# A four-layer graph network in fp32: one pool of 40 places for seven kinds of 4-KB buffers, row sums into a junk tile, and a plan taken strictly by a new table of due times

## The chip, the cores and the metric

The kernel runs on one core of a Trainium2 chip. Its engines are TensorE (PE, with its weight loads listed apart as PEld), VectorE (DVE), ScalarE (ACT), GpSimd (POOL) and SyncE (SP), which here only issues DMAs. The metric is the device time of one execution in microseconds (us). Before the change it was 2382.04, 2384.33 and 2385.14 us in three runs, with the median at 2384.33.

## The reference

There are 16 graphs of N = 1024 nodes with D = 128 features in fp32. `adj` is a weighted 1024 x 1024 adjacency matrix per graph. Four layers follow one another, each of them a layernorm with relu, a graph operation and a residual:

```python
# layer 0, three times (b is 0): cosine-weighted adjacency
h = h @ W + b
nh = h / jnp.maximum(jnp.linalg.norm(h, axis=-1, keepdims=True), EPS)
ew = adj * jnp.einsum('bij,bkj->bik', nh, nh)
h = jnp.einsum('bpq,bqc->bpc', ew, h)            # relu but for the last
# layer 1
h = (1.0 + eps) * x + jnp.einsum('bnf,bnm->bmf', x, adj)
y = jnp.maximum(h @ W1 + b1, 0.0) @ W2 + b2
# layer 2: attention with tanh scores
alpha = jnp.tanh(s1[:, :, None] + s2[:, None, :])
attn = jax.nn.softmax(jnp.where(adj > 0, alpha, NEG_INF), axis=-1)
last_h = jnp.einsum('bij,bjf->bif', attn, h)     # node itself where the row sum of adj is 0
# layer 3: gated attention
e = jnp.einsum('bil,bkl->bik', h @ A, h); e = e + jnp.swapaxes(e, 1, 2)
att = jax.nn.softmax(jnp.where(adj > 0, e, 0), axis=1) * adj
h_prime = jax.nn.relu(jnp.einsum('bij,bjk->bik', att, h))
out = o_c * jnp.tanh(jax.nn.sigmoid(i_c * h_prime + f_c * x))   # i_c, f_c, o_c: gates of [x, h_prime]
```

## The kernel before, in words

**Tiling.** The nodes lie in NB = 8 blocks of 128. A full feature tile is 128 partitions x 1024 elements: node blocks side by side, or, transposed, features on the partitions. Each graph keeps its adjacency transposed as eight tiles `adjT` of 128 x 1024, and reads it once more untransposed as tiles `adjL` for layer 1. A 512-element half of a row is the unit of the large products.

**A square.** Layers 0 and 3 need a symmetric 1024 x 1024 product of features (`sq`, class `Square`, L1335 to L1425). `row` (L1363) multiplies only from the diagonal block on; the blocks below are mirrored by transposes (`sq<-ident,above`, L1373) out of blocks kept in SBUF. `keep` stores them: ScalarE copies (L1398), or VectorE transposes (L1385) for a far quarter. Where a square is "by DMA", `send` writes a far quarter to DRAM (`by_hbm`, L1412) and fetches it turned (`got`, L1422). The kept blocks of one square are a tile `above` of 22 blocks (11 KB per partition).

**The stages of one graph.** Loads: `x` (L1459), for graph 0 untransposed chunks `raw` (L1494) that TensorE transposes (L1172), for the other graphs four DMAs per tile that fill `adjT` in 32 x 32 squares (L1518), VectorE's transpose of them (L1526) and ScalarE's row sum (L1529, eight tiles a graph for 15 graphs: 120). Layer 0, sublayers 00, 01, 02: projection `psP` (L1203), norms (square on ACT L1575, sum on DVE L1581, power -0.5 on POOL L1165, called `rn`), features transposed (`ps_hTn` L1172, evicted to `hTn` by L1225), square, `ew = sq*rn*adjT` on VectorE (L1598), product `acc0` (L1431), evicted by ScalarE to `hT` of the next sublayer (L1225). Layer 1: `adjL` plus the scaled identity (L1643), product with `hn`, two dense products. Layer 2: scores on ScalarE (L1764 and L1768), times adjT on VectorE (L1772, `e2`), product by nodes (L1442, `acc2`), and `hrow`, `pf` (L1706, L1713) for nodes alone. Layer 3: mask (L1842), masked scores with the maximum (L1863, `e3`), exp (L1895), times adjT on VectorE (L1904) or, in the last two graphs, in part on POOL (L1900), values `hs` scaled by the sums (L1909, L1913), product, `hpT` and `psN`, the gates (to L2008) and the output (L2015).

**The order.** Nothing is issued as it is written down. Each `pe`, `act`, `dve`, `pool_op` or `op("DMA", ...)` records an `Op` with an estimated duration in a `Plan` (from L57 on), with what it reads and writes. `Plan.order()` (L138 to about L220) then lists all of them, and they are emitted in that list's order under a manual schedule, so each engine's queue is the part of the list that is its own. SP has one queue for nearly all DMAs. Each operation has a due time, `batch * PERIOD + TIMES[key][nth]`, from a long table by stage, engine and tile, with entries of its own for the first two graphs and the last two. PERIOD is 145.06. `order()` steps through simulated time: of the operations that are ready it finds the earliest start, takes the engine of that start, and on this engine the one with the smallest due time within WINDOW = 0.05 us. While a VectorE operation with two SBUF inputs is planned, POOL operations are held off, and the other way round (`port`).

**Places.** A `Buf` takes a place in a pool when its first writer is listed; the place is free when its last user is. POOLS gives the places: adjT 16, adjL 5 (raw too), x 3, big 13 (`w4` work tiles and `chunk`s), above 2, and smaller ones. KINDS gives each kind its pool, the most places it may hold at once and the most that graphs later than the oldest unfinished one may hold. A reused place makes the new writer wait for the old users on the chip.

Of the kernel before, what the change touches and what calls it, by code (L numbers as in the profile page):

```python
# [10 lines left out]
I8 = mybir.dt.int8  # L11
AF = mybir.ActivationFunctionType
ALU = mybir.AluOpType
AX = mybir.AxisListType
# [20 lines left out]
class Buf:  # L35


    def __init__(self, kind, shape, name):
        self.kind, self.shape, self.name = kind, shape, name
        self.slot = self.t = None  # L40
        self.uses = 0
        self.seen, self.users = [], []
        self.end = 0.0
# [12 lines left out]
class Plan:  # L56
# [78 lines left out]
    def order(self):  # L135
# [12 lines left out]
        rows = {e: i for i, e in enumerate(self.LATENCY)}  # L148
        while ready:
# [4 lines left out]
            found = []  # L154
            for o in ready:
                if o.batch > oldest + self.ahead and o.engine != "DMA":
                    continue
                at = max(free[o.engine], o.from_)
                if o.port and port > at:
                    at = port  # L160
                if o.new:
                    need, room = {}, {}
                    for b in o.new:
                        need[b.kind] = need.get(b.kind, 0) + 1
                    for k, n in need.items():
                        pool, most, share = self.kinds[k]
                        if total[k] + n > most or (o.batch > oldest and young[k] + n > share):
                            at = None
                            break
                        room[pool] = room.get(pool, 0) + n  # L170
                    if at is not None:
                        for pool, n in room.items():
                            if len(state[pool]) < n:
                                at = None
                                break
                            at = max(at, state[pool][n - 1][0])
                    if at is None:
                        continue
                found.append((at, o))
            if not found:  # L180
                stuck = [b.name for o in ready if o.batch == oldest for b in o.new]
                raise RuntimeError(f"no slot for any of {stuck}")
            first = min(found, key=lambda f: (f[0], rows[f[1].engine]))
            at, o = min(
                (f for f in found if f[1].engine == first[1].engine and f[0] <= first[0] + self.window),
                key=lambda f: f[1].rank,
            )
# [34 lines left out]
def tile_adj_preln(  # L222
# [45 lines left out]
    nc.vector.memset(half, 0.5)  # L268
    mhalf = const.tile([P, NB], F32, name="mhalf")
# [55 lines left out]
    for load_it in first:  # L325
# [11 lines left out]
    POOLS = {"adjT": 16, "adjL": 5, "x": 3, "big": 13, "above": 2, "got": 1, "bank": 8, "small": 29, "row": 6, "hbm": 3, "hrow": 2, "mask": 5, "dot": 12}  # L337
    KINDS = {
        "adjT": ("adjT", 16, 16), "adjL": ("adjL", 5, 5), "x": ("x", 3, 3), "w4": ("big", 9, 5),
        "chunk": ("big", 10, 12), "above": ("above", 2, 1), "got": ("got", 1, 1), "ps": ("bank", 7, 8),  # L340
        "acc": ("bank", 7, 8), "small": ("small", 7, 16), "row": ("row", 3, 3), "hbm": ("hbm", 3, 3),
        "hrow": ("hrow", 1, 1), "mask": ("mask", 5, 5), "dot": ("dot", 6, 11),
    }
    PERIOD, AHEAD, WINDOW = 145.06, 2, 0.05

    TIMES = {
        "T DMA raw <0": [51.6, -92.65, -42.9, 3.5, 39.85, 7.55, 4, 14.6],
        "T PE raw <0": [8.95, 14, 0.9, 0.1, 1.8, 11.5, 24.3, 8.7, 10.25, 24.85, 23.15, 30.8, 27.8, 31.75,
            37.1, 39.05],
        "T ACT adjT <0": [10.4, 39.05, 8.5, 13.4, 18.8, 14.95, 18.55, 20.55, 23.6, 34, 35.15, 28.45, 39.25,  # L350
            43.8, 44.95, 62.3],
        "T DVE su <0": [53.8],
        "x DMA x <0": [51.55, -93.7],
        "0 DVE st <0": [3.5, 4.1],
        "0 DVE mv <0": [9.55],
        "0 POOL rstd <0": [4.05],
        "0 DVE nb <0": [8],
        "0 DVE hn <0": [9],
        "0 ACT hn <0": [38.8],
        "0 PE ps <0": [0.3, 12.55],  # L360
        "0 ACT hT <0": [-29.95, 13.25],
        "00 PE psP <0": [-4, -11.9],
        "00 DVE h <0": [12.3, 13.05],
        "00 PE ps <0": [23.7, 4.25],
        "00 ACT hTn <0": [15.5, 15.95],
        "00 ACT sq <0": [9.5, 16.45],
        "00 DVE ss <0": [-0.4, 17.4, 18.1],
        "00 POOL rn <0": [31.75],
        "00 PE sq <0": [5.9, 23.6, 7.2, 24.25, 13.15, 8.2, 10.5, -25.2, 6.35, 35.5, 21.75, 22.95, 30.8,
            27.05, 27.75, 40.9, 34.6, 52.3, 47.45, 25.15, 52.8, 47.65],  # L370
        "00 ACT above <0": [16.8, 25.9, 20.15, 21.45, 21.05, 27.1, 27, 35.15, 44.25, 39.55],
        "00 DVE ew <0": [20.55, 22.4, 22.5, 36.85, 24.55, 30.55, 38.4, 34.95, 29.5, 42.65, 33.2, 41.35, 48.7,
            51.6, 44.75, 54.3],
        "00 PE acc0 <0": [1.15, 16.5, 13, 10.35, 16.8, 17.8, 23.5, 23.4, 29.8, 44.65, 39.75, 41, 36.25,
            62.05, 45.45, 57.85],
        "00 POOL params <0": [36.5, 32.1, 45.3, 53, 56.95, 59.45, 57.95],
        "00 DMA params <0": [51.15],
        "00 DVE params <0": [65.55, 68.05, 68.05, 72.5, 77.85],
        "00 PE params <0": [46.25, 59.4, 67.2],
        "00 ACT hT <0": [71.35, 58.35],  # L380
        "01 PE psP <0": [48.7, 58.7],
        "01 DVE h <0": [69.85, 69.8],
        "01 PE ps <0": [62.15, 55.8],
        "01 ACT hTn <0": [74.6, 77.8],
        "01 ACT sq <0": [88.4, 75.85],
        "01 DVE ss <0": [76.35, 76, 75.35],
        "01 POOL rn <0": [85.7],
        "01 PE sq <0": [69.35, 77.1, 67.35, 71.05, 69.5, 61.9, 71.9, 72.55, 83.05, 79.35, 79.85, 82.25,
            81.65, 86.95, 89.5, 88.15, 86.6, 87.9, 88.85, 85.6, 88.85, 80.2],
        "01 ACT above <0": [84.55, 78.6, 81.55, 80.85, 88.55, 86.7, 99.05, 90.1, 98.25, 100.1],  # L390
        "01 DVE ew <0": [78.05, 92.3, 81.45, 86.7, 87.75, 96.2, 92.9, 91.6, 93.85, 100.95, 89.4, 98.6, 96.4,
            111.05, 92.4, 91.6],
        "01 PE acc0 <0": [73.8, 85.1, 79.95, 79.7, 80.75, 79.35, 85.55, 82.95, 86.65, 87, 85.75, 88.7, 88.55,
            92.6, 90.25, 95.7],
        "01 ACT hT <0": [102.35, 105.3],
        "02 PE psP <0": [93.5, 94.1],
        "02 DVE h <0": [111.55, 105.55],
        "02 PE ps <0": [95.75, 93.15],
        "02 ACT hTn <0": [114.45, 109.95],
        "02 ACT sq <0": [139.5, 103.55],  # L400
        "02 DVE ss <0": [110.85, 118.05, 110.75],
        "02 POOL rn <0": [132.95],
        "02 PE sq <0": [104.2, 101.25, 108.75, 111.1, 102.75, 106.15, 102.05, 93, 108.8, 109.9, 109.8, 115.1,
            115.55, 112.1, 119.5, 119.95, 122.9, 111.5, 118.6, 122.3, 121.85, 129.35],
        "02 ACT above <0": [114.75, 122.65, 108.55, 121.65, 119, 120.9, 125.85, 129.8, 136.8, 145.15],
        "02 DVE ew <0": [113.15, 105.5, 117.9, 112.35, 125.6, 119.95, 118.75, 124.8, 129.8, 126.4, 126.55,
            132.7, 131.6, 126.8, 122.9, 141.5],
        "02 PE acc0 <0": [115.6, 116.45, 107.95, 105, 109.15, 114.05, 117.4, 112.55, 132.75, 118.2, 123.05,
            131.2, 113.55, 121.5, 124.25, 117],
        "02 DVE x <0": [137.5, 138.95],  # L410
        "T DMA adjT <1": [-127.65, -137.2, -158.65, -112.3, -198.45, -149.5, -107.65, -98.7],
        "T DVE adjT <1": [-118.5, -112.1, -110.7, -105.6, -102, -90.25, -86.2, -85.25],
        "T ACT adjT <1": [-112.4, -112.9, -110.15, -106.5, -87.15, -73.4, -90.65, -89.55],
        "1 DVE st <0": [135.85, 142.2],
        "1 DVE mv <0": [141.85],
        "1 POOL rstd <0": [135.1],
        "1 DVE nb <0": [144.4],
        "1 DVE hn <0": [140.7],
        "1 ACT hn <0": [139.15, 139.6],
        "1 DVE x <0": [143.2, 166.35, 170],  # L420
        "1 DMA adjL <0": [51.6, 65.9, 63.85, 62.15, 49.9, 160.9, 153.9, 153.25],
        "1 DVE adjL <0": [80.75, 72.65, 82.35, 76.45, 78.15, 151.65, 156.4, 161.25],
        "1 PE acc1 <0": [135.6, 136.4, 137.3, 138.1, 140.45, 138.5, 143.45, 140.85, 143.9, 142.2, 148.6,
            147.5, 149.25, 146.5, 153.05, 144.3],
# [1712 lines left out]
```

## Time and profile before

| what | value |
|---|---|
| profiled execution | 2384.38 us |
| its span, first to last instruction | 2382.6 us |
| mean granted TensorE clock | 0.996 |
| median of three runs | 2384.33 us |
| DMA moved | 314.31 MB, mean 132 GB/s |
| largest group, DVE L1598 `ew<-sq,rn,adjT`, 612 x 739 ns | 439.2 us |
| row sums, ACT L1529, 120 x 1055 ns | 126.5 us |
| POOL power L1165 `rstd`, 64 x 1660 ns | 106.2 us |

The span is 1.8 us shorter than the execution's own time. A group's line of the profile has the source line, the engine, the operation and the tiles, the number of instructions, their busy time and mean, and then the engine's idle time just before them with what ended most of it. The slices of the span by tenths show the same level through the run except at its ends:

```profile
PE   8999999999999999999999999999999999999997
...
DVE  6658798998988989899898989989899898887676
ACT  7325765756566565765756567465765756655375
```

Each digit is one fortieth of the span (59.6 us).

### The profile page before, as it was taken

To read this page: it belongs to the slowest core of one execution; us is meant where nothing else is said; L and a number is where in the kernel's file an instruction comes from. 1 tells how busy PE (TensorE), PEld (TensorE's weight loads), DVE (VectorE), ACT (ScalarE), POOL (GpSimd) and SP (SyncE) were. 2 spreads that over 40 slices of the span, in tenths; PEclk is the share of its full clock that TensorE was granted. 3 is DMA by queue.
4 is the path that set the end of the run, shared out by engine and by line. 5 is a ranking of instruction groups with operands and counts; after the bars stand their busy time and mean duration, and the time that the engine had idled before them with its cause. 6 is when DMAs were issued, how large, how long until landed. Compare 5 with 4: busy or idle time off the path is not lost.

```text
span 2382.6 us, 35138 instructions
## 1 busy us (share of the span) xinstructions
PE 2346.0 (98%) x11577; PEld 1552.4 (65%) x11577; DVE 2038.7 (86%) x5570; ACT 1435.5 (60%) x2561; POOL 247.7 (10%) x168
## 2 busy tenths in 40 slices
PE   8999999999999999999999999999999999999997
PEld 5568566675757657566675766757576575765764
DVE  6658798998988989899898989989899898887676
ACT  7325765756566565765756567465765756655375
POOL 3001010100101101010100101001011100100012
PEclk9999999999999999999999999999999999999999
DMA  9332938668585875949769496775948768165000
GB/s 195 88 107 63 177 92 185 149 135 167 123 177 138 148 168 130 178 109 183 156 125 183 108 181 142 146 168 132 164 129 164 160 128 158 49 112 115 19 10 18
DMA packets 997254, 314.31 MB, mean 132 GB/s; under 512 B 682456, under 2 KB 978528, under 8 KB 997072
## 3 DMA queue, kind: packets, MB, share of 16 engines
q1 hardware_dynamic: 976912, 301.35, 61.0%
q10 hardware_dynamic: 19264, 9.70, 1.4%
q8 instruction: 92, 1.51, 0.3%
q0 software_dynamic: 896, 1.01, 0.2%
q14 instruction: 90, 0.74, 0.1%
HBM read 227.50 MB, written 84.47 MB: 131 GB/s over the span
## 4 chain that ended last, share of the span: by engine, by line
PE 95%; ACT 2%; DVE 1%; SPq 1%; DMA 1%; issue 0%; POOL 0%; DVEq 0%; ACTq 0%; POOLq 0%
PE acc L1431 36%; PE sq L1363 20%; PE acc L1442 19%; PE psP L1203 6%; PE sq L1373 4%; PE py L1660 2%; PE py L1213 2%; PE psN L1203 1%; PE pg L1213 1%; PE ps_hTn L1172 1%; SPq L1518 1%; PE ps_hnT L1172 1%; PE ps_h3T L1172 1%; DMA raw<-in_adj_dram 0%; ACT hT L1225 0%
## 5 line engine op out<-in xcount | busy, mean ns | idle before, releaser
L1598 DVE SCALAR_TENSOR_TENSOR ew<-sq,rn,adjT 128x512 f32<-128x512 f32 x612 | 439.2, 739 | 58.7 <-PE sq L1373 25.4
L1431 PE MATMUL acc<-ew,h 128*128 128x512 f32 x1024 | 484.4, 595 | 4.3 <-DVE ew L1598 4.3
L1363 PE MATMUL sq<-hTn 128*128 128x512 f32 (+3 forms) x1152 | 438.1, 489 | 0.8 <-ACT hTn L1225 0.5
L1398 ACT COPY above<-sq 128x384 f32<-128x384 f32 (+3 forms) x432 | 167.6, 392 | 353.7 <-PE sq L1373 260.5
L1363 PEld LDWEIGHTS sq<-hTn 128*128 128x128 f32 x1152 | 195.0, 191 | 144.7 <-issue 104.6
L1431 PEld LDWEIGHTS acc<-ew,h 128*128 128x128 f32 x1024 | 181.1, 191 | 162.3 <-issue 122.2
L1442 PEld LDWEIGHTS acc<-h,ew 128*128 128x128 f32 x2048 | 246.1, 192 | 35.6 <-issue 30.1
L1442 PE MATMUL acc<-h,ew 128*128 128x128 f32 x2048 | 252.8, 275 | 0.5 <-DVE ew L1598 0.5
L1442 PEld LDWEIGHTS acc<-h,e 128*128 128x128 f32 x2048 | 236.8, 192 | 22.6 <-issue 16.7
L1431 PE MATMUL acc<-e,hs 128*128 128x512 f32 x512 | 241.9, 593 | 4.4 <-ACT hs L1913 4.3
L1442 PE MATMUL acc<-h,e 128*128 128x129 f32 x2048 | 238.4, 275 | 1.9 <-DVE e L1772 1.9
L1165 POOL TENSOR_TENSOR rstd<-ve,mhalf 128x8 f32<-128x8 f32 x64 | 106.2, 1660 | 1228.4 <-DVE ve L1284 1228.3
L1431 PE MATMUL acc<-adjL,hn 128*128 128x512 f32 x512 | 232.7, 592 | 0.0
L1863 DVE CUSTOM_DVE_ANT_0 e<-mask,sq 128x512 f32<-128x512 int8 x204 | 136.2, 676 | 65.2 <-ACT above L1398 58.1
L1904 DVE TENSOR_TENSOR e<-e,adjT 128x512 f32<-128x512 f32 x248 | 162.7, 678 | 30.2 <-ACT e L1895 30.0
L1373 PEld LDWEIGHTS sq<-ident,above 128*128 128x128 f32 x960 | 124.4, 142 | 88.6 <-issue 71.2
L1529 ACT ACTIVATE adjT<-adjT 128x1024 f32<-128x1024 f32 x120 | 126.5, 1055 | 85.9 <-DVE adjT L1526 85.3
L1373 PE MATMUL sq<-ident,above 128*128 128x128 f32 x960 | 174.5, 274 | 0.0
L1385 DVE STREAM_TRANSPOSE above<-sq 128x512 f32<-128x512 f32 x208 | 146.0, 703 | 28.7 <-PE sq L1363 28.5
L1772 DVE SCALAR_TENSOR_TENSOR e<-adjT,e 128x512 f32<-128x512 f32 x256 | 163.0, 689 | 4.3 <-ACT e L1768 4.3
L1431 PEld LDWEIGHTS acc<-adjL,hn 128*128 128x128 f32 x512 | 93.6, 190 | 98.1 <-issue 86.2
L1431 PEld LDWEIGHTS acc<-e,hs 128*128 128x128 f32 x512 | 92.4, 190 | 98.5 <-issue 75.0
(164 smaller groups left out, 3645.7 us busy)
## 6 DMA issues: line engine op xcount, KB each, us to landing
adjL<-in_adj_dram SPq DMA_DIRECT2D x128, 512.0 KB
adjT<-in_adj_dram SPq DMA_DIRECT2D x480, 128.0 KB
by_hbm<-above SPq DMA_DIRECT2D x104, 512.0 KB
got<-by_hbm SPq DMA_DIRECT2D x416, 128.0 KB
s<-sd SPq DMA_DIRECT2D x15, 512.0 KB
out_dram<-z ACTq DMA_DIRECT2D x15, 512.0 KB
d_hT<-hn SPq DMA_DIRECT2D x14, 512.0 KB
hT<-d_hT SPq DMA_DIRECT2D x56, 128.0 KB
```

Of the source, the lines that this page charges most:

```text
L1203: nc.tensor.matmul(dst.t[:, (c - lo) * n : (c - lo + 1) * n], cols(srcT.t, c), w, start=True, stop=True)
L1363: lambda: nc.tensor.matmul(dst.t[:, (first - lo) * P :], cols(leftT.t, j), span(rightT.t, first, hi), start=True, stop=True),
L1373: nc.tensor.transpose(cols(dst.t, r), cols(above.t, p), ident)
L1385: lambda: nc.vector.transpose(self.apart(j // 2).rearrange("p (h r q i) -> p r h q i", r=2, q=QUARTER, i=SQ)[:, j % 2], read.t.rearrange(" ...
L1398: lambda: nc.scalar.copy(span(above.t, p, p + hi - first), read.t[:, (first - lo) * P :]),
L1431: lambda s=s, lo=lo, hi=hi: nc.tensor.matmul(acc[s].t, cols(h.t, at, w), span(ew.t, lo, hi), start=(j == 0), stop=(j == NB - 1)),
L1442: nc.tensor.matmul(a.t[:, (c - lo) * n : (c - lo + 1) * n], cols(ew.t, c), h.t[:, at * w : at * w + n], start=(j == 0 and c == lo), stop=( ...
L1529: lambda t=t, c=c: nc.scalar.activation(t.t, t.t, AF.Copy, accum_out=su.t[:, c : c + 1]),
L1598: lambda view=view, ew=ew, rn=rn, j=j, lo=lo, hi=hi: nc.vector.scalar_tensor_tensor(like(view(), span(ew.t, lo, hi)), view(), rn.t[:, j : ...
L1772: lambda e=e, j=j, lo=lo, hi=hi: nc.vector.scalar_tensor_tensor(span(e.t, lo, hi), span(aT[j].t, lo, hi), 0.0, span(e.t, lo, hi), op0=ALU. ...
L1863: lambda e=e, view=view, mask=mask, peak=peak, s=s, lo=lo, hi=hi: nc.vector.tensor_tensor_reduce(like(view(), span(e.t, lo, hi)), like(vie ...
L1904: lambda e=e, j=j, lo=lo, hi=hi: nc.vector.tensor_mul(span(e.t, lo, hi), span(e.t, lo, hi), span(aT[j].t, lo, hi)),
```

## The change

The list of operations that are recorded does not change. What changes is how they are ordered and where their buffers lie.

1. `order()` no longer looks for the earliest start. Of the ready operations it takes the one with the smallest due time of all engines whose buffers fit their limits; the simulated time is kept only to hand out places.
2. All of TIMES is new, and PERIOD is 144.24. POOL's durations count 8% more, some DMA durations are changed, and `dve()` and `pool_op()` no longer pass `port` on.
3. One pool "big" of 40 places serves adjT, adjL (and raw), x, w4, chunk and a new kind, quart; the title's seven kinds count raw by itself. Of a square's kept blocks, the six near the diagonal go to a tile `near` (3 KB) and each far pair of rows, eight blocks, to a `quart`. All limits in KINDS are new.
4. The row sum of `adjT` reads `adjT` and writes its full result to one int8 tile `unused`; before, it rewrote `adjT` in place.

```diff
-            found = []
-            for o in ready:
...
-            first = min(found, key=lambda f: (f[0], rows[f[1].engine]))
-            at, o = min(
-                (f for f in found if f[1].engine == first[1].engine and f[0] <= first[0] + self.window),
-                key=lambda f: f[1].rank,
-            )
+            o = next((o for o in sorted(ready, key=lambda o: (o.rank, o.seq)) if fits(o)), None)
...
-    POOLS = {"adjT": 16, "adjL": 5, "x": 3, "big": 13, "above": 2, "got": 1, "bank": 8, "small": 29, "row": 6, "hbm": 3, "hrow": 2, "mask": 5, "dot": 12}
+    POOLS = {"big": 40, "near": 2, "got": 1, "bank": 8, "small": 29, "row": 6, "hbm": 3, "hrow": 2, "mask": 5, "dot": 12}
     KINDS = {
...
+        "adjT": ("big", 17, 16), "adjL": ("big", 14, 4), "x": ("big", 7, 3), "w4": ("big", 21, 24),
+        "chunk": ("big", 9, 8), "near": ("near", 2, 1), "quart": ("big", 5, 8), "got": ("got", 1, 1),
...
-    PERIOD, AHEAD, WINDOW = 145.06, 2, 0.05
+    PERIOD, AHEAD, WINDOW = 144.24, 2, 0.05
...
-        return op("DVE", us + 0.015, reads, writes, fn, port)
+        return op("DVE", us + 0.015, reads, writes, fn)
...
-        return op("POOL", us, reads, writes, fn, True)
+        return op("POOL", us * 1.08, reads, writes, fn)
...
+            self.near = Buf("near", [P, 6 * P], f"near_{k}")
+            self.quart = [Buf("quart", [P, N], f"quart_{k}_{i}") for i in range(2)]
...
+        def place(self, r, c):
+
+            if r < QUARTER <= c:
+                return self.quart[r // 2], r % 2 * QUARTER + c - QUARTER
+            return self.near, PLACE[r, c]
...
-                S(N, False, True), [t], [t, su],
-                lambda t=t, c=c: nc.scalar.activation(t.t, t.t, AF.Copy, accum_out=su.t[:, c : c + 1]),
+                S(N, False, True), [t], [su],
+                lambda t=t, c=c: nc.scalar.activation(unused, t.t, AF.Copy, accum_out=su.t[:, c : c + 1]),
```

The diff also has code behind flags that are not set in this kernel (`squares_apart` with `mixed`, `one` and `some` behind "s"; the identity added to `adjL` on POOL behind "U"; another way of the gates behind "E"). None of it runs.

## The prediction

> **What bounds the kernel now.** I read the engines' shares first.
>
> ```profile
> PE 2346.0 (98%) x11577; PEld 1552.4 (65%) x11577; DVE 2038.7 (86%) x5570; ACT 1435.5 (60%) x2561; POOL 247.7 (10%) x168
> ...
> PE 95%; ACT 2%; DVE 1%; SPq 1%; DMA 1%; issue 0%; POOL 0%; DVEq 0%; ACTq 0%; POOLq 0%
> ```
>
> TensorE is busy for 98% of 2382.6 us and holds 95% of the chain that ended last. Here a rule speaks against reading 98% as "full": the Trainium skill ("Perfetto Trace Analysis", section "Identifying the Most-Contended Engine") says that [...]the weight loads' share should be read, which is 65% here. By the rule a third of the span, some 800 us, could be slack. So I took the spacing from each matmul's start to the next: the 128x512 records come every 0.429 us and the 128x128 ones every 0.111 us wherever nothing waits, and all records at such spacings make 2325 us. The row decides: about 39 us is lost between matmuls, 7.7 us lies before the first and 10.9 us after the last begins. No reordering can win more than about 57 us, and most of that only where those losses lie. The windows show where.
>
> ```profile
> 0.00:100.00 100.00, 87.87 (x381) 55.03 (x382) 65.32 (x169) 54.76 (x115) 27.41 (x40) 0.97 0.75 158
> ...
> 300.00:400.00 100.00, 99.09 (x530) 68.17 (x528) 92.83 (x244) 56.50 (x96) 12.00 (x7) 1.00 0.58 128
> 400.00:1900.00 1500.00, 1496.95 (x7274) 981.39 (x7273) 1347.85 (x3676) 934.94 (x1650) 139.33 (x85) 1.00 0.73 151
> ...
> 2300.00:2383.00 83.00, 64.86 (x323) 43.06 (x321) 61.83 (x186) 55.22 (x98) 18.02 (x9) 0.93 0.05 14
> ```
>
> The columns after the window are its length and then busy us of PE, PEld, DVE, ACT, POOL. 12 us are missing in the first window, 18 in the last, and only 3 in 1500 us of the middle. By spacing the middle loses 0.6 us per graph. The waits of TensorE name the owners.
>
> ```profile
> PE raw L1172 <- DMA raw<-in_adj_dram: 7.9, 2, 7.7
> PE acc L1431 <- DVE ew L1598: 4.3, 2, 4.0
> PE acc L1431 <- ACT hs L1913: 4.3, 2, 3.3
> PE psP L1203 <- ACT hT L1225: 3.0, 12, 0.3
> PE acc L1442 <- DVE e L1772: 1.9, 2, 1.6
> PE pf L1713 <- DVE hrow L1706: 1.1, 1, 1.1
> ```
>
> Only the fourth recurs: 12 times, once a graph. The others are head and tail.
>
> **What the change moves.** Every engine issues the same numbers and forms of instructions before and after (1385 DMA issues on SP and 166 instructions on POOL among them). So nothing is removed or added: the change is worth what the new order, places and waits are worth.
>
> *The recurring wait.* It is this place, once in most graphs:
>
> ```profile
> 1069.85 0.60 PE L1172 MATMUL ps_hTn<-ident,h 128*128 128x128 f32 x4
> 1070.05 0.60 ACT L1225 ACTIVATE hT<-acc 128x512 f32<-128x512 f32 x1
> ...
> 1070.70 2.94 PE L1203 MATMUL psP<-w,hT 128*128 128x128 f32 x24 [0.25 <-ACT hT L1225]
> ```
>
> The last accumulation of a sublayer ends, ScalarE moves it out in 0.60 us, and the next projection needs it; between them TensorE has only four transposes, 4 x 0.111 = 0.44 us. In the new order a projection of the next graph stands there instead: 4 matmuls of two records, 8 x 0.111 = 0.89 us. In the trace ScalarE ends 0.80 us after the transposes begin (1070.65 against 1069.85), and the next matmul starts 0.85 us after them. 0.89 just covers it. Measured by spacing, each case loses 0.41 us: 12 x 0.41 = **-4.9 us**. ScalarE's activation for the norm (L1575, 0.63 us), which stands directly ahead of that eviction now, comes after it in the new order, so nothing new is queued ahead of it.
>
> *The rest of the middle.* I walked TensorE's new queue with the old spacings and asked for each matmul how long before it the matmul that feeds its producer ends, less the producer's row. In graphs 2 to 12 the sum of negative margins falls from 4.0 us to 0. Other margins loosen (ew to acc from 1.72 us lead to 2.6 at the least); some tighten but stay positive (psN 1.72 to 1.53, ps_h3T 1.96 to 1.64). Some of the remaining 0.2 us per graph should go as well: **-1**. In 200 to 400 us the trace loses 5.5 us; one new short lead (psP of graph 2, 0.84 us) stands against one gone (0.15) and a looser load order: between -3 and +1, taken at **-1**.
>
> *Shared places.* adjT, adjL, x, the 4-KB work tiles, the raw chunks and the two far quarters of a square now draw on 40 places; the old split pools had 16+5+3+13 = 37, and "above" two of 11 KB apart. Steady adjL loads wait for places freed at 1085 to 1091 us of TensorE's work instead of 1095 to 1099, and are due at 1103 to 1110: their slack grows from 8.3-12.3 us to 16.6-17.6. The price: SP is one queue, and a load that waits for a place holds all behind it. In the new order adjT of the graph after next waits for acc0 of this one, ahead of the send and fetch of a square; the tile "got" that comes of them is used at least 10 us later than this wait ends. So **0**, and +0 to 4 if that cover is used up.
>
> *The row sums' junk tile.* 120 activations of 1.055 us (L1529) stay as many and as wide; I take the narrower int8 output at the same price, since ScalarE is 60% busy and no wait in the list names L1529. It frees readers of adjT from waiting for ScalarE, while the writes to one tile follow one another on the engine that runs them in order anyway: **0**; bounds -1 (head) to +1.
>
> *POOL and VectorE side by side.* The planner no longer keeps POOL's instructions apart from VectorE's with two SBUF inputs. In the old order 6 of 135 POOL instructions have such a neighbour within three; in the new one about 20, 13 of them the power for the next graph's norms (L1165, rn) beside e*adjT. The trace shows both outcomes:
>
> ```profile
> 2306.49 2.36 POOL L1900 TENSOR_TENSOR e<-e,adjT 128x1024 f32<-128x1024 f32 x1 [5.78 <-ACT e L1895]
> ...
> L1772 DVE SCALAR_TENSOR_TENSOR e<-adjT,e x256: 647/682/2868, 200.5 to 2322.7; 128x512 f32<-128x512 f32 x128
> L1165 POOL TENSOR_TENSOR rstd<-ve,mhalf x64: 1635/1636/2069, 7.6 to 2330.5; 128x8 f32<-128x8 f32 x64
> ```
>
> The 2868 ns (median 682) is the VectorE instruction that met that POOL one; in four cases it was the power that stretched, to at most 2069 ns, and VectorE's rows there are normal. The rule is harsher: the Trainium skill ("SBUF — State Buffer", section "Who interferes with whom") says that such a pair shares a port under an exclusive lock, whoever issues first. By the rule VectorE could lose the power's 1.64 us in each of 13 cases, 21 us of VectorE's time; by the row the power loses 0.43 us in each. I take the row, since it is the same instruction: the power is issued ahead of 4.9 us of VectorE work that precedes its first use, so **0**, with 0 to +21 as the ends.
>
> *Head.* SP is the limit: eight raw loads take 15.68 us of issue and 32 adjT issues 36.96 us, then two sends stand around an adjL issue, and TensorE waits 4.0 us for the ew of "got" at 69 us. New: the adjL issue (0.88 us) leaves that gap, the power and the first ew come about 1.6 us earlier, but TensorE has four transposes instead of sixteen to fill 8 to 18 us (+1 to 2). Waits of adjT loads for places clear within the first 5 us of TensorE's work, before SP reaches them. Sum between -4 and +2: **0**.
>
> *Tail.* The last 75 us hold the same groups in the new order. pf stands 58.2 instead of 65.4 us before the end of TensorE's work, so its wait for hrow (1.1 us, 1.4 by spacing; a row stretched by POOL) goes, as does a psN wait (0.7). What is late next there is the serial chain from the last layer-2 sum at 2324.6 to the first e3 at 2341.7, then 26 us of VectorE and 14.5 us of gates: all unchanged. -2.1, bounds -6 to +3: **-2**.
>
> Sum: -4.9 -1 -1 +0 -2 = -8.9. The profiled execution took 2384.38 us, the median of the runs is 2384.33, so one sum serves for both: **2375.4 us**.
>
> **Rivals.**
>
> *Nothing measurable* (within 0.2%, 4.8 us, about what a measurement of this kernel can tell): the 4.9 us come back as waits at the next thin place, for the 0.89 us lead has a margin of only 0.05. For it: one late ScalarE instruction suffices. Against: VectorE has 152 us of idle time in the middle's 1500. Then about 2382. Chance 0.18.
>
> *More*: loads released earlier and the new table also take half of the head's and tail's waits (11 + 13 us) and 200 to 400's: 2375.4 - 12 = 2363. For it: that is where the waits lie. Against: SP's issue rows and the serial chains are not shortened. 0.15.
>
> *Slower*: the port. Before ew of a new graph, VectorE now does 3.7 us of x and its statistics, which wait for the same accumulation that ends 4.2 us ahead of the matmul that needs ew: a margin of 0.3 to 0.6 us. If VectorE loses 1.64 us there, TensorE waits 1.64 - 0.45 = 1.2 us in each of 13 graphs, +15.5: 2375.4 + 15.5 = 2391. It decides once the block exceeds the margin. SP held for over 10 us by a place would be the same sign. 0.10.
>
> *The change does not do what it says*: the planner's times are not the chip's, and order by due time alone has no regard to an engine that stands ready; against it speaks that TensorE's queue is nearly the old one. Included in the second sign.
>
> The forecast has 0.57. With *more*, faster has 0.72; same 0.18; slower 0.10. The range drops half of *more* and of *slower*: 2364 to 2385.
>
> **What would show it.** The psP wait gone from TensorE's list (right) or still 12 times (wrong); the middle's loss at 0.1 to 0.3 us a graph; the e*adjT rows near 678 ns with powers near 2.0 us (port by the row) or e*adjT at over 2 us (by the rule); the ew wait near 69 us and the last 40 us as before. A new wait that recurs in each graph would prove me wrong, as would a first window with more than 90 us of TensorE.

## The result, and the profile after

The changed kernel took 2373.18 us (median; 2371.4 to 2375.19) against 2383.18 us of the kernel before in the same set of runs. The ratio is 0.9958, with a 95% interval of 0.9945 to 0.997: about 10 us faster. The profiled execution took 2375.19 us and its span is 2373.4 us, 9.2 less than before.

The engines' shares and the chain of waits of the changed kernel:

```profile
PE 2343.0 (99%) x11577; PEld 1551.8 (65%) x11577; DVE 2036.7 (86%) x5570; ACT 1445.6 (61%) x2561; POOL 253.4 (11%) x168
...
PE 95%; DVE 3%; DMA 1%; ACT 1%; SPq 0%; issue 0%; POOL 0%; ACTq 0%; DVEq 0%
```

The same instructions, the same bound, a shorter span. In the chain ScalarE falls from 2% to 1% and SP's queue from 1% to 0%, and VectorE rises from 1% to 3%. The windows of the changed kernel (length, busy us of PE, PEld, DVE, ACT, POOL, clock, DMA share, GB/s) show where TensorE lost less:

```profile
0.00:100.00 100.00, 91.16 (x406) 57.26 (x407) 65.42 (x151) 56.40 (x118) 25.60 (x39) 1.00 0.75 147
100.00:200.00 100.00, 97.65 (x493) 65.38 (x492) 64.34 (x189) 34.08 (x69) 8.49 (x6) 0.98 0.31 95
...
300.00:400.00 100.00, 99.30 (x531) 68.81 (x530) 92.49 (x246) 55.77 (x93) 12.30 (x7) 1.00 0.69 162
400.00:1900.00 1500.00, 1499.25 (x7295) 985.60 (x7294) 1348.57 (x3681) 945.01 (x1653) 143.85 (x84) 1.00 0.70 150
```

In 1500 us of the middle less than 1 us is missing, where 3 were. Busy time hides matmuls that ran slowly, so the sum is better made by spacing, as in the prediction: each start-to-start distance, less 0.429 us for a 128x512 record and 0.111 us for a 128x128 one.

| stretch, us of the span | lost before | lost after | difference |
|---|---|---|---|
| before the first matmul | 7.66 | 7.24 | -0.4 |
| 0 to 100 | 10.9 | 5.6 | -5.3 |
| 100 to 200 | 0.2 | 4.8 | +4.6 |
| 200 to 400 | 5.5 | 3.4 | -2.1 |
| 400 to 2200 | 9.2 | 3.7 | -5.6 |
| 2250 to the last matmul | 12.7 | 12.4 | -0.3 |

With -0.1 between 2200 and 2250, and 10.9 us after the last matmul begins in both, this is the -9.2 of the span. It compares one execution of each kernel. In the kernels e1_swap, e5_place, e9_place_all and e12_place_acc below, whose head is that of the kernel before, 0 to 100 us lose 8.5 to 10.4 us, and in e4_stats_later, e7_same and e8_tail, whose head is that of the changed kernel, 5.2 to 5.9. So 3 to 5 us is the safer figure for the head. The waits of TensorE name what is left:

```profile
PE raw L1178 <- DMA raw<-in_adj_dram: 7.2, 1, 7.2
PE acc L1478 <- DVE adjL L1696: 2.0, 1, 2.0
PE acc L1478 <- DVE top L1937: 1.5, 1, 1.5
PE psP L1249 <- ACT hT L1271: 1.4, 2, 0.8
```

The wait for ew at 69 us is gone, and the psP wait that came twelve times now comes twice. New is a wait of 2.0 us for `adjL`, which stands at 156 us. The recurring place now looks like this in the timeline of the changed kernel (start, duration, engine and line):

```profile
1063.22 1.24 DVE L1202 STREAM_TRANSPOSE hT<-hT 128x1024 f32<-128x1024 f32 x1
...
1065.39 2.01 PE L1249 MATMUL psP<-w,hT 128*128 128x128 f32 x16
1065.60 0.60 ACT L1271 ACTIVATE hT<-acc 128x512 f32<-128x512 f32 x1 [4.11 <-PE acc L1478]
...
1067.24 0.60 PE L1178 MATMUL ps_hTn<-ident,h 128*128 128x128 f32 x4
```

The eviction of `hT` ends at 1066.20. TensorE's 16 records from 1065.39 on are the next graph's projection, whose features VectorE turned by 1064.46, and then the projection that needs the eviction, with no wait between: the first eight end at 1066.28 by spacing, 0.08 us behind the eviction. But the four transposes, which stood ahead of the projections before, come behind them too: more was moved here than the one block.

### The profile page after: what moved, and what is told of

It reads as the page before. It is cut to its first block, busy times and chain, and to the rows that moved or that the text cites. A ratio compares the mean times of both kernels' runs of the same rounds, so it can differ in the third digit from the quotient of the medians.

```text
span 2373.4 us, 35020 instructions
## 1 busy us (share of the span) xinstructions
PE 2343.0 (99%) x11577; PEld 1551.8 (65%) x11577; DVE 2036.7 (86%) x5570; ACT 1445.6 (61%) x2561; POOL 253.4 (11%) x168
## 4 chain that ended last, share of the span: by engine, by line
PE 95%; DVE 3%; DMA 1%; ACT 1%; SPq 0%; issue 0%; POOL 0%; ACTq 0%; DVEq 0%
PE acc L1478 36%; PE sq L1415 20%; PE acc L1489 19%; PE psP L1249 6%; PE sq L1425 4%; PE py L1713 2%; PE py L1259 2%; PE ps_hTn L1178 1%; PE pg L1259 1%; PE psN L1249 1%; DVE e L1957 1%; DVE e L1916 1%; PE ps_hnT L1178 1%; PE ps_h3T L1178 1%; DMA x<-in_x_dram 1%; DVE e L1825 0%
## 5 line engine op out<-in xcount | busy, mean ns | idle before, releaser
L1645 DVE SCALAR_TENSOR_TENSOR ew<-sq,rn,adjT 128x512 f32<-128x512 f32 x612 | 432.4, 738 | 69.8 <-PE sq L1425 40.7
L1478 PE MATMUL acc<-ew,h 128*128 128x512 f32 x1024 | 476.6, 593 | 0.3 <-DVE ew L1645 0.3
L1415 PE MATMUL sq<-hTn 128*128 128x512 f32 (+3 forms) x1152 | 430.2, 487 | 0.4 <-ACT hTn L1271 0.4
L1450 ACT COPY near<-sq 128x128 f32<-128x128 f32 (+2 forms) x384 | 140.0, 367 | 325.5 <-PE sq L1425 256.3
L1825 DVE SCALAR_TENSOR_TENSOR e<-adjT,e 128x512 f32<-128x512 f32 x256 | 162.7, 684 | 12.4 <-ACT e L1821 12.0
L1948 ACT ACTIVATE e<-e,top 128x1024 f32<-128x1024 f32 x128 | 146.6, 1146 | 41.4 <-DVE top L1937 40.0
L1957 DVE TENSOR_TENSOR e<-e,adjT 128x512 f32<-128x512 f32 x248 | 169.1, 701 | 2.5 <-ACT e L1948 2.5
L1171 POOL TENSOR_TENSOR rn<-ss,mhalf 128x8 f32<-128x8 f32 x48 | 83.3, 1736 | 817.3 <-DVE ss L1632 700.1
L1425 PEld LDWEIGHTS sq<-ident,near 128*128 128x128 f32 x768 | 101.4, 141 | 81.8 <-issue 56.0
L1817 ACT ACTIVATE e<-s,h 128x1024 f32<-128x1024 f32 x128 | 143.8, 1139 | 13.4 <-DMA s<-sd 13.4
```

Source lines behind the costliest of these rows:

```text
L1171: pool_op(1.64, [src], [dst], lambda: nc.gpsimd.tensor_tensor(dst.t, src.t, mhalf, op=ALU.pow))
L1415: lambda: nc.tensor.matmul(dst.t[:, (first - lo) * P :], one(leftT, j), some(rightT, first, hi), start=True, stop=True),
L1425: nc.tensor.transpose(cols(dst.t, r), cols(kept.t, p), ident)
L1478: lambda s=s, lo=lo, hi=hi: nc.tensor.matmul(acc[s].t, cols(h.t, at, w), span(ew.t, lo, hi), start=(j == 0), stop=(j == NB - 1)),
L1645: lambda view=view, ew=ew, rn=rn, j=j, lo=lo, hi=hi: nc.vector.scalar_tensor_tensor(like(view(), span(ew.t, lo, hi)), view(), rn.t[:, j : ...
L1817: lambda e=e, j=j: nc.scalar.activation(e.t[:, 0:N], s1.t[:, 0:N], AF.Tanh, bias=h.t[:, j * E2 + D + 1 : j * E2 + D + 2]),
```

## The experiments

Experiments that reorder move operations in the finished list after `ordered = plan.order()`. In the diffs `which(key, graph, nth)` names an operation, and `ahead` and `behind` put it there. Each ratio is against the kernel before of the same set of runs, with its 95% interval.

**Only the cover of the recurring wait (e1_swap), in the kernel before.**

```diff
     ordered = plan.order()
+    for g in range(1, B - 2):
+        first, then = which("00 PE psP", g + 1, 0), which("02 PE psP", g, 1)
...
+            ahead(first, then)
```

> The kernel before, with one move: in 12 graphs the next graph's first projection (4 matmuls) is issued ahead of the projection that waits for ScalarE's hT, instead of behind it. Theory A (the recurring wait is worth what the spacing says): the 12 waits of psP for hT go, TensorE's loss between 400 and 1900 us falls from about 7 to about 2 us, and the time from 2383.2 to 2378.3. Theory B (the freed time comes back at the next thin place): other waits take over, and the time stays within 1 us of 2383.2.

It took 2384.28 us, 1.0007 (1.0 to 1.0013). The psP wait for `hT` is no longer in TensorE's list, yet nothing is won. The timeline shows the new holder:

```profile
1069.26 1.24 DVE L1194 STREAM_TRANSPOSE hT<-hT 128x1024 f32<-128x1024 f32 x1
...
1070.60 2.13 PE L1203 MATMUL psP<-w,hT 128*128 128x128 f32 x17
```

The block moved up needs features that VectorE turns only until 1070.50; TensorE stood for 0.22 us and then lost 0.3 more at the transposes' evictions and the square behind them. In all 0.7 us per graph are lost there, about what the old wait and its surroundings cost.

**The places split again by kind (e2_split, e10_split18), in the changed kernel**: 40 places still, in four pools, with the limits in KINDS to match.

```diff
-    POOLS = {"big": 40, "near": 2, ...
+    POOLS = {"adjT": 16, "adjL": 5, "x": 3, "big": 16, "near": 2, ...      # e2_split
+    POOLS = {"adjT": 18, "adjL": 5, "x": 3, "big": 14, "near": 2, ...      # e10_split18
...
```

> The changed kernel with the 40 places split again (adjT 16, adjL 5, x 3, the rest 16), new table and strict rule kept; TensorE's order differs in a few dozen rows. Theory A (the gain comes of the order): 2373.2, within 2 us. Theory B (the shared places bring it, through earlier loads): most of the 10 us is lost, 2380 or more, with TensorE waiting for DMA or for adjL.

> The changed kernel with its 40 places split as adjT 18, adjL 5, x 3 and 14 for the rest; the order differs from the changed kernel's in some rows on every engine. Theory A (in e2 it was adjT alone, whose loads waited for e*adjT of the graph before and held SP's queue): most of e2's 75 us is gone, 2373 to 2385. Theory B (the sharing of all kinds is needed): 2420 or more.

They took 2457.7 us, 1.0318 (1.0304 to 1.0332), and 2461.15 us, 1.0338 (1.0322 to 1.0353). The waits of SP's DMA queue in e2_split begin with

```profile
SPq L1565 <- DVE e L1957: 343.9, 81, 25.0
```

where the same line of the changed kernel reads

```profile
SPq L1565 <- PE acc L1478: 69.1, 28, 8.3
```

and with two more places for adjT, in e10_split18, the queue waits at the loads of adjL instead:

```profile
SPq L1523 <- PE acc L1478: 205.7, 54, 15.1
```

where that line of the changed kernel has 67.5 us. L1565 issues the adjT loads and L1523 those of adjL. With 16 places, adjT of a graph to come waits until layer 3 has multiplied by its predecessor, up to 25 us at once, and SP's one queue holds every later DMA meanwhile. What is issued late comes late to VectorE. In e2_split it waits

```profile
DVE adjT L1573 <- DMA adjT<-in_adj_dram: 75.3, 23, 5.9
DVE adjL L1696 <- DMA adjL<-in_adj_dram: 50.6, 26, 8.5
```

where the changed kernel has neither wait, and TensorE's largest wait in the steady graphs is then one for VectorE (18.3 us in 18 pieces). In e10_split18 the two waits of VectorE are 17.8 and 47.2 us: given to adjT, the same places are missed by others. So the new order lives on places that any kind may take: without them it is 75 to 79 us slower than before (medians less 2382.48 and 2382.11 of their sets), in either division that was tried. The planner's order shifts in some rows with each division, so the places are not wholly apart from the order here. What the new pools do for the old order was not tried.

**The row sums alone (e3_inplace, e11_junk_before).** The changed kernel with its sums written back in place, in the same order, and the kernel before with a junk tile.

```diff
-                lambda t=t, c=c: nc.scalar.activation(unused, t.t, AF.Copy, ...   # e3_inplace
+                lambda t=t, c=c: nc.scalar.activation(t.t, t.t, AF.Copy, ...
-                lambda t=t, c=c: nc.scalar.activation(t.t, t.t, AF.Copy, ...      # e11_junk_before
+                lambda t=t, c=c: nc.scalar.activation(unused, t.t, AF.Copy, ...
```

> The changed kernel with the row sums written back to adjT instead of the junk tile, in the same order on every engine. Theory A (the junk tile is worth nothing, since the sums stand long before their readers' need): 2373.2, within 1 us. Theory B (readers of adjT were held by the rewriting): 2 to 6 us longer, with new waits of DVE or PE for ACT L1576.

> The kernel before with the row sums' result in a junk tile, in the same order on every engine. Theory A (worth nothing): within 1 us of before. Theory B (readers of adjT gain): 2 us or more below.

e11_junk_before took 2381.49 us, 0.9999 (0.999 to 1.0007): at the order of the kernel before the junk tile is worth nothing.

e3_inplace took 2376.55 us, 0.9977 (0.9967 to 0.9986), with a span of 2373.3. Its interval overlaps that of the changed kernel, so the times alone cannot tell them apart, though its median is 3.4 us higher. Its profile does show a price: VectorE has a wait that neither profile of the changed kernel has, 13 times:

```profile
DVE ew L1645 <- ACT adjT L1576: 8.6, 13, 3.4
```

VectorE has to wait until ScalarE has rewritten `adjT`. After the longest of these waits, which ends at 254 us, VectorE is busy without a break, and TensorE waits 1.2 us for it at 260 us. By spacing e3_inplace loses 29.8 us, the profile after 29.9; but the latter has two stretches at half clock (see e7_same), and e3_inplace has none before its end. Against e7_same, which has none either, its span is 3.5 us longer (2373.3 and 2369.8). So in the new order the junk tile is likely worth about 3 us, with one profile on each side. What it allows the planner, to order without regard to the write, was not tried apart.

**The new stall at 156 us (e4_stats_later), in the changed kernel.** The timeline shows how it comes about:

```profile
146.08 0.63 ACT L1375 ACTIVATE hn<-hn 128x512 f32<-128x512 f32 x1 [15.73 <-DVE hn L1347]
146.15 0.38 ACTq L1506 DMA_DIRECT2D x<-in_x_dram  x1
...
154.62 1.65 DVE L1319 BATCH_NORM_STATS2 st<-x 128x6 f32<-128x128 f32 x8 [4.99 <-DMA x<-in_x_dram]
...
156.51 8.83 PE L1478 MATMUL acc<-adjL,hn 128*128 128x512 f32 x16 [1.96 <-DVE adjL L1696]
```

The brackets give the idle time before an instruction and who ended it. The load of `x` for graph 2 is issued by ScalarE behind an activation that waited 15.73 us. VectorE's statistics of that `x` wait 4.99 us for it, and behind them stand the additions to `adjL` of graph 0, on which TensorE then waits.

```diff
     ordered = plan.order()
+    adds = [which("1 DVE adjL", 0, j) for j in range(NB)]
+    for n in (1, 0):
+        behind(which("0 DVE st", 2, n), *adds)
```

> The changed kernel with one move on VectorE's queue: the statistics of graph 2's x, which wait for a late load, are issued behind the last four additions of the identity to graph 0's adjL instead of ahead of them. Theory A (that wait in VectorE's queue makes the new stall at 156 us, and TensorE pays 2.1 us for it and 1.7 to 2 us at half clock after it): TensorE's loss between 150 and 200 us falls from 4.8 to about 0.7, and the time from 2373.2 to 2369. Theory B (adjL itself is late): the stall stays, no change within 1 us.

It took 2371.16 us, 0.9955 (0.9942 to 0.9969). The wait for `adjL` is gone, the loss in 150 to 200 us falls from 4.8 to 0.9, and the span is 2369.4, 4.0 less than that of the profile after. The median is only 2 us lower, within the intervals. The cause of the stall is shown by the profile; that the repair helps is not shown by the times alone.

**The transposes moved as well (e5_place), in the kernel before**: VectorE turns the next graph's features before the first half of `h`, and both projections go ahead of the four transposes, as the new order has it.

```diff
+        put(flip_hT[0], min(ordered.index(flip_hT[0]), ordered.index(which("02 DVE h", g, 0))))
+        ahead(first, turned_h)
...
+        ahead(then, turned_h)
```

> The kernel before with all three moves of the new order at the recurring place, in 12 graphs: VectorE transposes the next graph's features ahead of (not behind) the first half of h, and TensorE issues the next graph's projection and then this graph's own ahead of the four transposes. Theory A (e1 failed only because the projection that was moved up had to wait for that transposition on VectorE): the place loses under 0.15 us a graph instead of 0.6, and the time is 5 to 7 us shorter, about 2377. Theory B (that graph's work is late everywhere by then, and any order moves the wait): within 1.5 us of before.

It took 2411.31 us, 1.0116 (1.0103 to 1.013): 27 us slower, which neither theory had. TensorE's waits:

```profile
PE sq L1363 <- ACT hTn L1225: 19.1, 14, 1.6
PE psP L1203 <- ACT hT L1225: 9.3, 13, 0.7
```

Each comes once a graph. VectorE makes the first half of `h` later now, ScalarE's square of it (L1575) waits for that and stands ahead of the eviction of `hT` in ScalarE's queue, and the evictions of `hTn` come later still.

**ScalarE's order too (e9_place_all), then TensorE's as well (e12_place_acc)**, each on top of the one before: the squares for the norm behind both evictions of `hTn`, layer 3's `hn` ahead of them, the sums behind them; then the last row of the square ahead of the first accumulations.

```diff
...
+            behind(which("02 ACT sq", g, 1), taken[1])               # e9_place_all
...
+        behind(squared, taken[1])
+        for side in (1, 0):                                          # e12_place_acc
+            o = next(o for o in ordered if any(t.name == f"sq_{g}_2_3_{side}" for t in o.new))
...
+                ahead(o, acc_first)
```

> The kernel before with the moves of e5 and those of ScalarE and VectorE that stand with them in the new order: ScalarE evicts hT ahead of the squares for the norm, does layer 3's hn next and both halves of hTn, then the squares; VectorE sums the squares behind both halves of h. Theory A (in e5 the square's activation, held by the later h, stood ahead of the eviction that TensorE waits for): the place loses under 0.15 us a graph, and the time is 5 to 7 us below before, about 2377. Theory B (the place can't be mended alone, since norms and ew behind it come too late): 0 or more above before, with the loss at acc or sq behind the place.

> The kernel of e9 with one more piece of the new order on TensorE: the products for the fourth row of the square are issued ahead of the first accumulations of that sublayer instead of behind them, in 12 graphs (0.5 us of TensorE's work more between the norms and their first user). Theory A (e9's remaining wait, for VectorE's sums at L1585, is only the short cover between the square and the accumulations): that wait goes, the middle loses under 0.3 us a graph, and the time is 4 to 6 us below before, about 2378. Theory B (the wait only moves on again, to a psum bank or to ew): 2382 or more.

They took 2384.95 us, 1.0012 (1.0006 to 1.0019), and 2385.53 us, 1.0015 (1.0008 to 1.0021). The long waits of e5_place and the old psP wait are gone, and a new one stands in each list, eleven times, first in e9_place_all:

```profile
PE acc L1442 <- DVE ss L1585: 3.9, 11, 0.4
```

and then, moved on once more, in e12_place_acc:

```profile
PE sq L1363 <- DVE ss L1585: 3.8, 11, 0.4
```

The profile names the sum `ss`, which ends within 0.1 us of the first `ew`. The power `rn` now comes late, with it the first `ew`, and with that the bank that it frees. In e12_place_acc `rn` starts 2.91 us after the square's first matmul (1075.05 less 1072.14), in the changed kernel 2.49 (1071.50 less 1069.01), where two of ScalarE's squares stand between the two evictions of `hTn` and not behind both. That last difference was not tried.

**The head alone (e6_head), in the kernel before**: three of the eight raw chunks take free places of adjT instead of waiting for an adjL place, and the adjL load no longer stands between the two sends.

```diff
+    ahead(which("1 DMA adjL", 0, 0), which("1 DMA adjL", 0, 1))
...
+    for c in range(5, NB):
+        t, later = places[f"raw_0_{c}"], places[f"adjT_1_{c}"]
+        t.pool, t.slot = later.pool, later.slot
```

> The kernel before with two changes of its head: three raw chunks lie in places that graph 1's adjT takes later, so that they wait for no place, and the first adjL load is issued behind the two sends of graph 1's far quarters instead of between them. Theory A (the head's gain comes of the fetch of got being earlier): got's last fetch is issued about 2.5 us earlier (62.2 instead of 64.7 us), the loss between 50 and 100 us falls from 7.4 to 4 or 5, and the time by 2.5 to 3.5. Theory B (the gain is TensorE's order, which has other work for the wait): under 1.5 us.

It took 2378.03 us, 0.9976 (0.9967 to 0.9985), 5.8 us less than the kernel before (2383.83). SP's queue in the timeline of e6_head:

```profile
1.22 13.14 SPq L1494 DMA_DIRECT2D raw<-in_adj_dram  x8
...
55.87 3.81 SPq L1422 DMA_DIRECT2D got<-by_hbm  x8
```

The raw loads are issued in 13.14 us instead of 15.68, and the fetch of `got` ends at 59.68 instead of 64.67 us. By spacing, 50 to 100 us lose 1.2 instead of 7.4. So borrowed places and one load moved are worth something by themselves at one spot, the head; which of the two edits brings how much was not tried.

**The changed kernel once more (e7_same).** No edit; it asks how much of a profile's loss is its own.

> The changed kernel itself again, on the chip of the others of this set, for comparison: 9 to 10 us below before, 2373.

It took 2375.43 us, 0.9964 (0.9951 to 0.9978). Its profiled span is 2369.8, 3.6 us less than that of the other profile of the same code, with the same stall of 2 us at 156 us. What differs is the clock. In these traces the granted clock changes only at steps of 3.41 us. The step with the stall and the one behind it, in the first profile and in this one (busy us of PE come after the length, the clock is the third number from the end):

```profile
154.08:157.50 3.42, 1.46 (x6) 0.58 (x5) 2.88 (x13) 0.37 (x1) 0.00 (x0) 1.00 0.43 152
157.50:160.91 3.41, 3.41 (x6) 1.34 (x5) 3.25 (x19) 0.00 (x0) 1.64 (x1) 0.50 0.00 1
```

```profile
154.06:157.47 3.41, 1.76 (x4) 0.87 (x5) 3.41 (x21) 0.00 (x0) 0.00 (x0) 1.00 0.50 154
157.47:160.88 3.41, 3.41 (x9) 1.52 (x8) 2.48 (x13) 0.00 (x0) 1.64 (x1) 1.00 0.00 0
```

In the first execution the whole stall lies in one step, and the next step runs at half clock; in the second the stall begins in the step before, and the clock stays. The same happens near the end, where the first profile has another step of 0.50, from 2352.26 us, and the second has not. Half of two steps is 3.4 of the 3.6 us.

**The end (e8_tail), in the changed kernel**, with the edit of e4_stats_later. Two of the lines of its end as it was, from the changed kernel's timeline:

```profile
2345.90 2.90 POOL L2046 TENSOR_TENSOR z<-z,x 128x1024 f32<-128x1024 f32 x1
2345.92 3.43 DVE L1957 TENSOR_TENSOR e<-e,adjT 128x512 f32<-128x512 f32 x2
```

They start together, and one of the two VectorE instructions took 2844 ns where the median is 682. The edit holds POOL's last addition until the last `e*adjT` is done, by a product of one column that reads its result, and sends the output by SP.

```diff
+    behind(held, last)
...
+    def held_add():
+        nc.gpsimd.tensor_tensor(spare, e_last.t[:, 0:1], mhalf[:, 0:1], op=ALU.mult)
+        add_x()
```

> The changed kernel with the move of e4 and one more: POOL's last addition for graph 14's output waits, by a one-column POOL product with a junk result, until VectorE's last e*adjT of graph 15 is done, and that output is sent from SP's queue. Theory A (this POOL instruction stretched an e*adjT of graph 15 to 2.84 us at 2346 us, and TensorE paid for it with a stall of 1.7 us and as much at half clock): 3 us below e4, 2366, no e*adjT over 0.7 us after 2340 us. Theory B (VectorE's sum of work sets the end): under 1 us below e4.

It took **2367.89 us** (2367.45 to 2368.24), 0.9934 (0.9922 to 0.9947). This beats both kernels: by 15.9 us the kernel before (2383.83), and by 7.5 us the changed kernel of the same set (2375.43), whose interval lies apart from this one. In its timeline the addition stands at

```profile
2351.88 2.35 POOL L2046 TENSOR_TENSOR z<-z,x 128x1024 f32<-128x1024 f32 x1
```

and no `e*adjT` after 2340 us takes more than 0.68 us. By spacing, 2300 to 2350 us lose 4.6 instead of 6.6, and the rest 0.1 instead of 1.9. How the 7.5 us divide between the two edits is not measured by times; it is more than the two stalls (2.0 and 1.5 us of waiting), and in the profiles the halved clock behind each goes as well.

## Why the prediction was right, and where it was not

The forecast was 2375.4 us and the median 2373.18; the profile's difference is -9.2 against a sum of -8.9. The total is that close by luck: two misses of opposite sign, in the head and at 156 us, cancel.

**The recurring wait and the rest of the middle** (-4.9 and -1): measured -5.6 in 400 to 2200 us, or 0.74 to 0.30 us per graph (1800 us are 12.4 graphs). The size was right. The cover as put, 0.89 us of other matmuls over ScalarE's 0.80, stands in the changed kernel and just suffices there, but alone it is not enough: e1_swap puts the same block ahead of the waiting projection and wins nothing. The next thin place holds TensorE instead, which was the rival "nothing measurable", and it is true of every partial move: e1_swap, e9_place_all and e12_place_acc end 2 to 3 us above the kernel before in their sets, e5_place 27. In the changed kernel the features are turned earlier, the projections stand ahead of the transposes, and ScalarE, POOL and VectorE have the order that goes with it. So the gain comes only with more of the new order than any piece that was tried. Which further pieces are needed stays open, and the new rule of `order()`, the new table and POOL's 8% were not tried apart.

**200 to 400 us** (-1): measured -2.1, within the bounds given.

**Head** (0, from -4 to +2): here the step failed, and two of the prediction's own signs say so: the first window has 91.16 us of TensorE, over the 90 that were to prove it wrong, and the wait for ew near 69 us, which was to stay, is gone. The prediction saw that the adjL issue leaves the gap of the sends, and set +1 to +2 for lost transposes against it. The loss in 0 to 100 us fell by 5.3 and the first matmul came 0.4 earlier. Two terms were mis-sized. The prediction took the 15.68 us of raw issue as SP's fixed price, but part of it goes when the chunks find other places: in the changed kernel the eight issues take 12.70 us, in e6_head, where three of them do, 13.14. And the 4.0 us of the ew wait carried more with it: in 69 to 75 us the clock in the profile of the kernel before was 0.54, which went with the wait. That much was this execution's; with the same head e12_place_acc has 0.80 there. e6_head wins 5.8 us by these two edits alone.

**The stall at 156 us** (not in the sum): +4.6, of which 1.7 is the half clock of that execution. The walk through the queues asked what each matmul's producer had waited for on TensorE, not what stood ahead of it on VectorE and waited for a DMA that ScalarE issued late. e4_stats_later shows the cause.

**Shared places** (0): as a price of waiting this was right, since no wait of SP's queue reached TensorE in the steady graphs. As a worth it was wrong: the new order rests on them, and without them it loses 75 us and more. The hold of SP's queue, which the prediction weighed as a danger, is what the shared places prevent for the loads of adjT and adjL.

**The junk tile** (0, from -1 to +1): right for the old order, by e11_junk_before. In the new order it was likely too small: e3_inplace speaks for about 3 us, through the readers of `adjT` that the prediction named and put at nothing.

**Port** (0, up to +21): right in the middle, not at the end. In the changed kernel the groups read

```profile
L1171 POOL TENSOR_TENSOR rn<-ss,mhalf x48: 1637/1637/2611, 17.6 to 2214.1; 128x8 f32<-128x8 f32 x48
...
L1957 DVE TENSOR_TENSOR e<-e,adjT x248: 643/682/2844, 239.1 to 2357.3; 128x512 f32<-128x512 f32 x124
```

with minimum, median and maximum in ns. Eleven powers beside an `e*adjT` stretched to 1.94 to 2.61 us, somewhat more than the 2.07 taken from the trace of before, and the `e*adjT` beside them kept 0.68. One such pair, and then a pair near the end with TensorE behind it:

```profile
963.13 0.68 DVE L1957 TENSOR_TENSOR e<-e,adjT 128x512 f32<-128x512 f32 x1
963.31 2.01 POOL L1171 TENSOR_TENSOR rn<-ss,mhalf 128x8 f32<-128x8 f32 x1 [33.31 <-DVE ss L1632]
...
2290.66 2.84 POOL L1953 TENSOR_TENSOR e<-e,adjT 128x1024 f32<-128x1024 f32 x1 [4.40 <-ACT e L1948]
2291.28 2.78 DVE L1957 TENSOR_TENSOR e<-e,adjT 128x512 f32<-128x512 f32 x1
...
2294.11 1.13 PE L1478 MATMUL acc<-e,hs 128*128 128x512 f32 x2 [1.00 <-DVE e L1957]
```

The prediction set row against rule, but both outcomes fit the rule of the Trainium skill ("SBUF — State Buffer", section "Who interferes with whom"), that the order of issue decides who is blocked. Each of the eleven powers waits for a sum that stands just ahead of the `e*adjT` in VectorE's queue, so VectorE is in that product 0.17 to 0.24 us before the power starts, and the power is the one that is late. At 2290.66 POOL stood first, and VectorE lost, 2.78 us for 0.68. That is a cost of the change that the prediction put at nothing: TensorE waits 1.0 us for this product, and 1.5 us at 2352 us behind the one of 2844 ns. e8_tail shows that the second could be had back.

**Tail** (-2): -0.3. The waits for `hrow` and `hpT` are off the list as forecast, and 2300 to 2350 us lose 2.0 less; but 2250 to 2300 us lose 1.5 more (3.9 for 2.4), where TensorE now waits for ScalarE's `h` (1.4) and VectorE's `e` (1.0 and 0.8), and the rest 0.2 more. "All unchanged" did not hold for the groups before the chain. The 1.0 is the wait at 2294.11 above, behind a product that POOL held up; what makes ScalarE's `h` late was not tried.

## What to carry to other kernels

In this kernel, where every engine runs a planned order close to its limit, a wait of 0.4 us that recurs was a property of the order: four attempts to cover it at its place moved it on, and only the new order of all engines removed it. So look, before such an edit, at what the other engines do in the next few us. Large waits at the head and the end were different: a few local edits in one or two queues won 5.8 us in the head of the kernel before and 7.5 us in the changed one. Before splitting or sharing buffers, look at what a load that waits for a place holds behind it on the one queue that issues.

## What the runs showed of the hardware that was not expected

A short stall of TensorE can cost twice, and whether it does depends on where it falls. The stall of 4.0 us in the kernel before was followed by a clock of 0.54 for 6 us. The one of 2 us at 156 us was followed by half clock for 3.41 us in one execution and by none in another of the same code, a difference of about 1.7 us each time it happened. The Trainium skill ("TensorE: Matmul & The Clock Gate", section "HAM oscillation — how this bites in real kernels") speaks of idle gaps above about 3.4 us; here 2.0 us was enough where it lay in one step of 3.41 us, and in e11_junk_before a stall of 3.3 us, ended at 67 us, was not: it was split over two steps, each with over 1.5 us of work, and the clock of 69 to 75 us stayed at 1.00. In the 14 kept traces, with each step's work counted in matmuls at the spacing above, every full-clock step with less than 1.18 us of it was followed by half clock and none with more than 1.32; between the two, both occur.

Which of POOL and VectorE loses when they meet depended on which had started: the same kind of product on VectorE kept 0.68 us in one place and took 2.78 in another of one run (963 and 2291 us of the profile after).
